# The end of an adaLN block: transposes of the last layernorm in another bank, the down product by four tiles, and a new order of the last block

## The chip, the cores and the metric

The kernel runs on one core of one Trainium2 chip. A core has five engines, each with its own queue of instructions: TensorE (PE; its weight loads are shown apart as PEld), VectorE (DVE), ScalarE (ACT), GpSimd (POOL) and SyncE (SP, which here only issues transfers). Engines wait for each other through semaphores. The metric is the device time of one execution in microseconds (us); of several runs the median is given. Three runs of the kernel before took 1085.74, 1085.96 and 1087.61 us, so its median is 1085.96 us.

## The reference

One transformer block in fp32 with adaptive layernorm, on x of shape (2, 1024, 256). From a small vector c come six rows per batch: shifts and scales for two layernorms, and two gates.

```python
h = _layernorm(x, axis=-1) * (1 + ca) + sa
x = x + ga * attention(h)          # 16 heads of 128, rotary positions, causal softmax, biases
h = _layernorm(x, axis=-1) * (1 + cb) + sb
x = x + gb * ffn(h)
```

The feed-forward part is `down(silu(gate(h)) * up(h))` with a hidden width of 704; its three weights are integers with a zero point and a scale per row. 704 is five chunks of 128 and one of 64.

## The kernel before, in words

**The main loop.** A unit is one head of one batch; there are 32. For each unit the loop projects q, k and v, forms the causal scores of eight query tiles of 128 rows in two-bank tiles of PSUM (pool `ps_sc`, two buffers), takes the softmax on VectorE and ScalarE, transposes the probabilities, multiplies by v and adds the output projection to x, which stays in SBUF. Nothing of this loop is touched by the change. The order of all work is written out by hand (`tc.manual_schedule`, L646): each engine executes its instructions in the order in which the Python code emits them, and the framework adds the waits.

**The end.** After the last unit (from L737) the two batches go through the feed-forward part in four blocks of 512 rows, named (batch, block): (0,0), (0,1), (1,0), (1,1). What a block needs:

- Layernorm: `ln_stats`, `ln_sqrt`, `ln_scale` give normalised tiles `xn_b` (128 rows by 256). `ln_turn` (L206) turns four of them: for each half f of the 256 columns four transposes on TensorE (L210) into one bank of `ps_a`, then one VectorE instruction (L217) that scales and shifts into h. It is called for the blocks (1,0) and (1,1) at the end, and twice, with ScalarE for the second half, at the kernel's start.
- `hidden(b, blk, c)` (L525) computes chunk c of the hidden layer: gate and up products (L538) into one two-bank tile `pgu` of `ps_sc`, a SiLU on ScalarE (L557), a product on VectorE (L558) into `gT`. The sixth chunk (c = 5) holds gate in 64 rows and up in the other 64 of one product, and its VectorE work (L553) writes even row tiles to partitions 0 to 63 of `gT` and odd ones to 64 to 127.
- `down(b, blk, *js)` (L560) forms the output of row tiles js: for each tile five products over 128 rows (L566), then for all js one product over the remaining 64 rows (L575, on the lower or the upper 64 rows of the array by the tile's parity), then an addition of x on VectorE (L588) into a tile `yo` and a store issued by SP (L589). The `yo` tiles of block (0,0) come from a pool of two buffers, all others from the pool of `xn`, with four.

**Banks.** `bank` (L496) hands out single banks in turn: `ps_y`, `ps_o`, `ps_a`, `ps_a`. The late output projections (`project_out(..., late=True)`, whose reader on VectorE is L512) and all `pd` tiles of `down` use it. `ps_a` has two buffers, which `ln_turn` uses as well.

**The order at the end.** `hidden(0,1,5)`; `ln_turn` for (1,0); statistics of the last four tiles; `down(0,0)` of tiles 0 and 1; `ln_scale`; `down(0,0)` of tiles 2 and 3; `ln_turn` for (1,1); then the six chunks of (1,0) with `down(0,1)` of all four tiles behind chunk 3; the six chunks of (1,1) with `down(1,0)` behind chunk 3; `down(1,1)` in two pairs of tiles.

Of the kernel before, what the change touches and what calls it, by code (L numbers as in the profile page):

```python
# [11 lines left out]
F32 = mybir.dt.float32  # L12
I32 = mybir.dt.int32
AF = mybir.ActivationFunctionType
ALU = mybir.AluOpType
PSUM = bass.MemoryType.PSUM

P = 128
B, S, D = 2, 1024, 256
H, DH = 16, 128  # L20
HID = 704
NT = S // P
KC = D // P
HG = 2
NG = H // HG
NF = (HID + P - 1) // P
FULL = (HID // P) * P
QB = 512
# [9 lines left out]
def adaln_block(ctx: ExitStack, tc: tile.TileContext, a, cos_d, sin_d, out):  # L38
    nc = tc.nc
# [4 lines left out]
    xnp = pool("xn", 4)  # L44
    fpool = pool("f", 2)
    rot = pool("rot", 2)
    ps_a = pool("ps_a", 2, space=PSUM)
    ps_o = pool("ps_o", 1, space=PSUM)
    ps_y = pool("ps_y", 1, space=PSUM)
    ps_sc = pool("ps_sc", 2, space=PSUM)  # L50
# [3 lines left out]
    x = [const.tile([P, NT, D], F32, name=f"x{b}") for b in range(B)]  # L54
    x_d = a["L0_attn_x"]
    R_BQ, R_BK, R_BV = 0, H, 2 * H
    cols = const.tile([P, 3 * H], F32, name="cols")
    sc = const.tile([P, B, KC], F32, name="sc")
# [8 lines left out]
    for n in range(KC):  # L67
        load_x(0, 2 * n, 2, nc.sync)
        half = slice(n * D, (n + 1) * D)
# [3 lines left out]
    ident = const.tile([P, P], F32, name="ident")  # L73
# [10 lines left out]
    for n in range(3):  # L84
# [10 lines left out]
        out=mask[:, NT - 1, :],  # L95
# [92 lines left out]
    def ln_sqrt(b, name, t0, t1):  # L188
        mv, rstd = stats[b, name]
        nc.scalar.activation(rstd[:, t0:t1], mv[:, t0:t1, 1], AF.Sqrt, bias=eps_t)  # L190

    xns = {}

    def ln_scale(b, name, blk, part=range(4)):
        mv, rstd = stats[b, name]
        part = [4 * blk + j for j in part]
        some = slice(part[0], part[-1] + 1)
        nc.vector.reciprocal(rstd[:, some], rstd[:, some])
        for t in part:
            xn = xnp.tile([P, D], F32, tag="xn", name=f"xn_{name}{b}_{t}")  # L200
            nc.vector.tensor_scalar(
                xn, x[b][:, t, :], mv[:, t, 0:1], rstd[:, t : t + 1], ALU.subtract, ALU.mult
            )
            xns[b, name, t] = xn

    def ln_turn(b, name, blk, which, dest, split=False):  # L206
        for f in range(KC):
            pt = ps_a.tile([P, 512], F32, tag="a", name=f"ptx_{name}{b}_{blk}_{f}")
            for j in range(4):
                nc.tensor.transpose(  # L210
                    pt[:, ts(j, P)], xns[b, name, 4 * blk + j][:, ts(f, P)], ident
                )
            shift, scale = (modT[:, which + n, f, b : b + 1] for n in range(2))
            if split and f:
                nc.scalar.activation(dest[:, f, :], pt, AF.Identity, bias=shift, scale=scale)
            else:
                nc.vector.tensor_scalar(dest[:, f, :], pt, scale, shift, ALU.mult, ALU.add)  # L217

    moved = {}

# [34 lines left out]
    wdT = [const.tile([P, NF, D], F32, name=f"wdT{b}") for b in range(B)]  # L255
# [240 lines left out]
    def bank(name):  # L496

        pool, tag = banks[turn[0] % 4]
        turn[0] += 1
        return pool.tile([P, 512], F32, tag=tag, name=name)  # L500
# [16 lines left out]
    h2s, gTs = {}, {}  # L517

    def new_h2(b, blk):

        tag = (f"hT{blk}", f"cs{blk}")[b]
        h2s[b, blk] = hpool.tile([P, KC, QB], F32, tag=tag, name=f"h2_{b}{blk}")
        return h2s[b, blk]

    def hidden(b, blk, c, late=True):  # L525
        if c == 0:
            gTs[b, blk] = fpool.tile([P, NF, QB], F32, tag="f", name=f"gT_{b}{blk}")
        last = c == NF - 1
        if late:
            pg = ps_sc.tile([P, S], F32, tag="sc", name=f"pgu_{b}{blk}{c}")  # L530
            pgs = [pg[:, ts(j, QB)] for j in range(2)]
        else:
            pgs = [
                ps_a.tile([P, 512], F32, tag="a", name=f"pgu_{b}{blk}{c}{j}") for j in range(2 - last)
            ]
        for pg, n in zip(pgs, ("gate",) if last else ("gate", "up")):
            for k in range(KC):
                nc.tensor.matmul(  # L538
                    pg,
                    wT["last"][:, k, :] if last else wT[n][:, k, ts(c, P)],  # L540
                    h2s[b, blk][:, k, :],
                    start=(k == 0),
                    stop=(k == KC - 1),
                )
        sg = ppool.tile([P, QB], F32, tag="p", name=f"sg_{b}{blk}{c}")
        if last:

            m = HID - FULL
            nc.scalar.activation(sg[m:], pgs[0][:m], AF.Silu)

            for j, rows_ in enumerate((slice(0, m), slice(m, P))):
                part = lambda t: t.rearrange("p (t j q) -> p t j q", j=2, q=P)[:, :, j, :]
                nc.vector.tensor_tensor(  # L553
                    part(gTs[b, blk][rows_, c, :]), part(sg[m:]), part(pgs[0][m:]), ALU.mult
                )
        else:
            nc.scalar.activation(sg, pgs[0], AF.Silu)  # L557
            nc.vector.tensor_tensor(gTs[b, blk][:, c, :], sg, pgs[1], ALU.mult)  # L558

    def down(b, blk, *js):  # L560

        pds = {}
        for j in js:
            pds[j] = bank(f"pd_{b}{blk}{j}")
            for c in range(NF - 1):
                nc.tensor.matmul(  # L566
                    pds[j][:, :D],
                    gTs[b, blk][:, c, ts(j, P)],
                    wdT[b][:, c, :],
                    start=(c == 0),  # L570
                    stop=False,
                )
        for j in js:
            half = ts(j % 2, HID - FULL)
            nc.tensor.matmul(  # L575
                pds[j][:, :D],
                gTs[b, blk][half, NF - 1, ts(j, P)],
                wdT[b][half, NF - 1, :],
                start=False,
                stop=True,  # L580
            )
        for j in js:
            t = blk * 4 + j
            if (b, blk) == (0, 0):
                yo = rot.tile([P, D], F32, tag="r1", name=f"yo_{b}{t}")
            else:
                yo = xnp.tile([P, D], F32, tag="xn", name=f"yo_{b}{t}")
            nc.vector.tensor_tensor(yo, pds[j][:, :D], x[b][:, t, :], ALU.add)  # L588
            nc.sync.dma_start(out[b, ts(t, P), :], yo)  # L589


    units = [(b, g, h) for b in range(B) for g in range(NG) for h in range(HG)]
# [53 lines left out]
    with tc.manual_schedule():  # L646
# [30 lines left out]
        ln_scale(0, "a", 0, (2, 3))  # L677
        shift_scale(0)
        ln_turn(0, "a", 0, 0, new_hT(0, 0), split=True)
        for t in range(4, NT):  # L680
            ln_stats(0, "a", t)
# [5 lines left out]
        ln_scale(0, "a", 1)  # L687
        release()
        ln_turn(0, "a", 1, 0, new_hT(0, 1), split=True)
        gates()  # L690
        for s in ("q", "k"):
# [3 lines left out]
        for n, u in enumerate(units):  # L695
            b, g, h = u
# [4 lines left out]
            for i in range(NT):  # L701
# [26 lines left out]
                if not nxt and i < NF:  # L728
                    hidden(0, 0, i, late=False)
# [9 lines left out]
        for c in range(4):  # L739
            hidden(0, 1, c)  # L740
            project_out(prev, 4 + c, late=True)
            project_out(u, c, late=True)
# [4 lines left out]
        values(u, 1, 0, 8)  # L747
        ln_scale(1, "b", 0)
        hidden(0, 1, 4)
        for t in range(4, NT):  # L750
            project_out(u, t, late=True)
        hidden(0, 1, 5)
        ln_turn(1, "b", 0, 2, new_h2(1, 0))
        for t in range(4, NT):
            ln_stats(1, "b", t)
        ln_sqrt(1, "b", 4, NT)
        down(0, 0, 0, 1)
        ln_scale(1, "b", 1)
        down(0, 0, 2, 3)
        ln_turn(1, "b", 1, 2, new_h2(1, 1))  # L760
        for c in range(NF):
            hidden(1, 0, c)
            if c == 3:
                down(0, 1, 0, 1, 2, 3)
        for c in range(NF):
            hidden(1, 1, c)
            if c == 3:
                down(1, 0, 0, 1, 2, 3)
        down(1, 1, 0, 1)
        down(1, 1, 2, 3)  # L770


def _rotary_tables():
# [65 lines left out]
```

## Time and profile before

| what | value |
|---|---|
| median of three runs | 1085.96 us (1085.74 to 1087.61) |
| the profiled execution's own time | 1085.72 us |
| its span in the profile | 1083.9 us |
| TensorE busy | 1072.0 us, 99% of the span |
| VectorE, ScalarE, GpSimd busy | 60%, 47%, 37% |
| granted TensorE clock | 1.00 |
| the four blocks' end, from `ln_turn` for (1,0) on | 999.73 to 1083.9 us |

The profile is of one execution. A row of a timeline gives its start and its length in us, the engine, the line of the kernel, the operation with what it writes and reads, how many instructions are merged in it, and in brackets how long the engine stood idle before and for whom. [...] the pace of TensorE is the distance from one start to the next. An fp32 product is two records in the trace, each with a weight load of its own.

### The profile page before, as it was taken

What the parts mean: (1) busy time and instruction counts of PE and PEld (TensorE: products, weight loads), DVE (VectorE), ACT (ScalarE), POOL (GpSimd) and SP (SyncE); (2) the same over time, 40 slices, a digit from 0 to 9 for tenths busy, and PEclk for the clock granted to TensorE, in tenths of its full rate; (3) what the DMA queues carried; (4) which work ended last, traced back from release to release, by engine and by line L of the source; (5) the groups of instructions that cost most, each with busy time, mean ns of one, the idle gap of its engine ahead of it and who ended that gap; (6) DMA issues with size and microseconds to landing.
All of it is one profiled execution on the core that took longest, in us unless ns stands there. A gap on an engine that the chain in (4) does not pass through costs nothing.

```text
span 1083.9 us, 12352 instructions
## 1 busy us (share of the span) xinstructions
PE 1072.0 (99%) x3524; PEld 638.7 (59%) x3524; DVE 655.5 (60%) x1422; ACT 507.6 (47%) x956; POOL 397.2 (37%) x364
## 2 busy tenths in 40 slices
PE   8999999999999999999999999999999999999998
PEld 5556555566666556556566666665655566555656
DVE  5566566767677856556656665666677766454321
ACT  4645445455445444445455444454445445652110
POOL 4635353535343343664343433333333334100000
PEclk9999999999999999999999999999999999999999
DMA  6355656657564556555564645454556556422001
GB/s 211 81 140 132 159 141 137 168 116 182 127 150 96 131 120 151 126 128 143 111 148 106 151 109 141 101 138 101 142 117 153 117 123 143 97 66 51 20 20 39
DMA packets 67191, 130.97 MB, mean 121 GB/s; under 512 B 18962, under 2 KB 23314, under 8 KB 67124
## 3 DMA queue, kind: packets, MB, share of 16 engines
q1 hardware_dynamic: 64772, 125.91, 49.1%
q10 hardware_dynamic: 2304, 4.16, 1.2%
q8 instruction: 28, 0.46, 0.2%
q14 instruction: 39, 0.32, 0.1%
q0 software_dynamic: 48, 0.13, 0.1%
HBM read 25.26 MB, written 2.10 MB: 25 GB/s over the span
## 4 chain that ended last, share of the span: by engine, by line
PE 95%; DVE 2%; SPq 1%; DMA 1%; ACT 1%; issue 0%; DVEq 0%; ACTq 0%
PE po L483 23%; PE ps L422 22%; PE pk L379 10%; PE pq L379 10%; PE py L509 10%; PE pv L361 10%; PE pgu L538 6%; PE pd L566 3%; SPq L468 1%; DMA pT<-t 1%; DMA wmod<-in_wmod 0%; PE pd L575 0%; ACT L557 0%; DVE ps L425 0%; DVE t L456 0%
## 5 line engine op out<-in xcount | busy, mean ns | idle before, releaser
L442 ACT ACTIVATE p<-ps,nmax 128x128 f32<-128x128 f32 (+7 forms) x256 | 189.8, 741 | 421.6 <-DVE nmax L425 421.5
L422 PE MATMUL ps<-kT,qT 128*128 128x512 f32 (+3 forms) x768 | 289.5, 486 | 0.7 <-ACT p L442 0.7
L425 DVE CUSTOM_DVE_ANT_0 ps<-ps,mask 128x128 f32<-128x128 f32 (+7 forms) x256 | 195.6, 764 | 132.9 <-PE ps L422 132.6
L483 PE MATMUL po<-pT,v 128*128 128x512 f32 (+3 forms) x768 | 264.0, 487 | 1.7 <-DMA pT<-t 1.6
L512 DVE SCALAR_TENSOR_TENSOR x<-py,rden,x 128x256 f32<-128x256 f32 x256 | 123.0, 482 | 182.9 <-PE py L509 176.2
L483 PEld LDWEIGHTS po<-pT,v 128*128 128x128 f32 x768 | 145.2, 190 | 133.0 <-issue 107.5
L456 DVE STREAM_TRANSPOSE t<-p 128x128 f32<-128x128 f32 (+7 forms) x256 | 198.1, 774 | 0.4 <-ACT p L442 0.4
L422 PEld LDWEIGHTS ps<-kT,qT 128*128 128x128 f32 x768 | 145.7, 190 | 77.5 <-issue 62.9
L392 POOL TENSOR_TENSOR r_k<-r_k,sin_t 128x512 f32<-128x512 f32 x64 | 81.4, 1272 | 223.0 <-ACT r_k L391 222.9
L509 PE MATMUL py<-wo,o 128*128 128x256 f32 x512 | 151.5, 380 | 1.4 <-DVE x L512 1.4
L392 POOL TENSOR_TENSOR r_q<-r_q,sin_t 128x512 f32<-128x512 f32 x64 | 81.7, 1276 | 140.3 <-ACT r_q L391 137.3
L398 POOL TENSOR_TENSOR kT<-kT,r_k 128x512 f32<-128x512 f32 x64 | 81.3, 1270 | 140.9 <-DVE rden L506 101.5
L509 PEld LDWEIGHTS py<-wo,o 128*128 128x128 f32 x512 | 92.3, 190 | 67.3 <-issue 51.2
L361 PE MATMUL pv<-wv,hT 128*128 128x256 f32 x512 | 121.0, 379 | 1.1 <-DVE qT L395 1.1
L379 PE MATMUL pq<-hT,wq 128*128 128x512 f32 x256 | 120.6, 593 | 0.5 <-DVE hT L217 0.5
L379 PE MATMUL pk<-hT,wk 128*128 128x512 f32 x256 | 120.3, 592 | 0.0
L361 PEld LDWEIGHTS pv<-wv,hT 128*128 128x128 f32 x512 | 94.9, 190 | 19.9 <-DVE qT L395 1.2
L391 ACT ACTIVATE r_q<-pq,cols 64x512 f32<-64x512 f32 x128 | 87.4, 683 | 20.9 <-PE pq L379 19.2
L398 POOL TENSOR_TENSOR qT<-qT,r_q 128x512 f32<-128x512 f32 x64 | 83.6, 1306 | 31.1 <-DVE qT L395 28.6
L391 ACT ACTIVATE r_k<-pk,cols 64x512 f32<-64x512 f32 x128 | 87.4, 683 | 6.2 <-PE pk L379 0.4
L379 PEld LDWEIGHTS pk<-hT,wk 128*128 128x128 f32 x256 | 48.6, 190 | 54.6 <-issue 44.0
L379 PEld LDWEIGHTS pq<-hT,wq 128*128 128x128 f32 x256 | 46.1, 190 | 33.8 <-issue 31.2
(89 smaller groups left out, 688.8 us busy)
## 6 DMA issues: line engine op xcount, KB each, us to landing
pT<-t SPq DMA_DIRECT2D x512, 128.0 KB, 2.4
pT<-t SPq DMA_DIRECT2D x512, 64.0 KB, 2.0
wq<-in_Wq SPq DMA_DIRECT2D x16, 256.0 KB, 3.1
wk<-in_Wk SPq DMA_DIRECT2D x16, 256.0 KB, 4.0
wv<-in_Wv SPq DMA_DIRECT2D x16, 256.0 KB, 4.2
wo<-in_Wo SPq DMA_DIRECT2D x16, 256.0 KB, 2.9
out<-yo SPq DMA_DIRECT2D x16, 128.0 KB, 1.8
x<-in_x SPq DMA_DIRECT2D x4, 256.0 KB, 5.4
```

The source lines that it names most:

```text
L361: nc.tensor.matmul(pv[:, ts(j, HG * DH)], hT[b, n][:, k, ts(r, P)], weights[b, g]["v"][:, k, :], start=(k == 0), stop=(k == KC - 1),)
L379: nc.tensor.matmul(pq, weights[b, g][s][:, k, ts(h, DH)], hT[b, n][:, k, :], start=(k == 0), stop=(k == KC - 1),)
L391: nc.scalar.activation(r1[to], pq[of], AF.Identity, bias=cols[of, c : c + 1])
L392: nc.gpsimd.tensor_tensor(r1, r1, sin_t[:, sl], ALU.mult)
L398: nc.gpsimd.tensor_tensor(dst[:, sl], dst[:, sl], r1, ALU.add)
L422: nc.tensor.matmul(ps[:, c:e], qT[:, ts(i, P)], kT[:, c:e], start=True, stop=True)
L425: nc.vector.tensor_tensor_reduce(ps[:, :L], ps[:, :L], mask[:, NT - 1 - i :, :].rearrange("p t k -> p (t k)"), -SCALE, FLT_MAX, ALU.add, A ...
L442: nc.scalar.activation(p[:, :L], ps[:, :L], AF.Exp, bias=nmax, scale=-1.0, accum_out=dens[u][:, i : i + 1])
L456: nc.vector.transpose(t32[blk][:, :, j, : i + 1, :].rearrange("p c k b -> p k c b"), p[:, : (i + 1) * P].rearrange("p (k c a) -> p k c a", ...
L483: nc.tensor.matmul(po[:, off * P :], vs[b, g][:, k, ts(h, DH)], pT[:, off:, :, k, :], start=(k == 0), stop=(k == last),)
L509: nc.tensor.matmul(py[:, :D], outs[u][:, ts(t, P)], weights[b, g]["o"][:, h, :], start=True, stop=True)
L512: nc.vector.scalar_tensor_tensor(x[b][:, t, :], py[:, :D], rdens[u][:, t : t + 1], x[b][:, t, :], ALU.mult, ALU.add)
```

## The change

It has four parts.

1. `ln_turn` can take one two-bank tile of the scores' pool (`wide`) in place of two banks of `ps_a`; the call for (1,0) does. In all calls both halves' tiles are now taken first, and the readers are emitted behind all eight transposes.
2. `down` treats all four row tiles in one call, for every block. Block (0,0) was done in two pairs before; `ln_scale` of the last four tiles now stands ahead of it.
3. `ln_turn` for (1,1) is called behind chunk 0 of (1,0) and not ahead of it.
4. In block (1,1) chunk 5 of the hidden layer is computed first, `down(1,0)` follows the third further chunk in that order, and `down(1,1)` starts with the 64-row products of all tiles. Each tile then gets its five 128-row products, its addition and its store before the next tile is begun. The fourth tile is split into two parts of 128 columns, the second in a bank of the scores' pool; each part has its own addition and store.

```diff
-    def ln_turn(b, name, blk, which, dest, split=False):
+    def ln_turn(b, name, blk, which, dest, split=False, wide=False):
+        tag = f"ptx_{name}{b}_{blk}"
+        if wide:
+            both = ps_sc.tile([P, S], F32, tag="sc", name=tag)
+            pts = [both[:, ts(f, QB)] for f in range(KC)]
+        else:
+            pts = [ps_a.tile([P, 512], F32, tag="a", name=f"{tag}_{f}") for f in range(KC)]
         for f in range(KC):
-            pt = ps_a.tile([P, 512], F32, tag="a", name=f"ptx_{name}{b}_{blk}_{f}")
             for j in range(4):
                 nc.tensor.transpose(
-                    pt[:, ts(j, P)], xns[b, name, 4 * blk + j][:, ts(f, P)], ident
+                    pts[f][:, ts(j, P)], xns[b, name, 4 * blk + j][:, ts(f, P)], ident
                 )
+        for f in range(KC):
...
-    def hidden(b, blk, c, late=True):
-        if c == 0:
+    def hidden(b, blk, c, late=True, first=None):
+        if c == 0 if first is None else first:
...
-    def down(b, blk, *js):
+    def down(b, blk):
+
+        end = (b, blk) == (1, 1)
+        pds = [bank(f"pd_{b}{blk}{j}") for j in range(4)]
+
+        parts = [(j, pds[j], slice(0, D)) for j in range(4)]
+        if end:
+            rest = ps_sc.tile([P, S], F32, tag="sc", name=f"pd_{b}{blk}r")
+            parts[3:] = [(3, pds[3], slice(0, P)), (3, rest, slice(P, D))]
+
+        def halves():
+            for j, pd, cols in parts:
+                half = ts(j % 2, HID - FULL)
+                nc.tensor.matmul(
+                    pd[:, cols],
+                    gTs[b, blk][half, NF - 1, ts(j, P)],
+                    wdT[b][half, NF - 1, cols],
+                    start=end,
+                    stop=not end,
+                )
+
+        def chunks(j, pd, cols):
             for c in range(NF - 1):
                 nc.tensor.matmul(
-                    pds[j][:, :D],
+                    pd[:, cols],
                     gTs[b, blk][:, c, ts(j, P)],
-                    wdT[b][:, c, :],
-                    start=(c == 0),
-                    stop=False,
+                    wdT[b][:, c, cols],
+                    start=(c == 0 and not end),
+                    stop=(c == NF - 2 and end),
                 )
...
+        def store(j, pd, cols):
             t = blk * 4 + j
...
+            nc.vector.tensor_tensor(yo[:, cols], pd[:, cols], x[b][:, t, cols], ALU.add)
+            nc.sync.dma_start(out[b, ts(t, P), cols], yo[:, cols])
+
+        yos = {}
+        if end:
+
+            halves()
+            for part in parts:
+                chunks(*part)
+                store(*part)
+            return
+        for part in parts:
+            chunks(*part)
+        halves()
+        for part in parts:
+            store(*part)
...
-        ln_turn(1, "b", 0, 2, new_h2(1, 0))
+        ln_turn(1, "b", 0, 2, new_h2(1, 0), wide=True)
         for t in range(4, NT):
             ln_stats(1, "b", t)
         ln_sqrt(1, "b", 4, NT)
-        down(0, 0, 0, 1)
         ln_scale(1, "b", 1)
-        down(0, 0, 2, 3)
-        ln_turn(1, "b", 1, 2, new_h2(1, 1))
+        down(0, 0)
         for c in range(NF):
             hidden(1, 0, c)
+            if c == 0:
+                ln_turn(1, "b", 1, 2, new_h2(1, 1))
             if c == 3:
-                down(0, 1, 0, 1, 2, 3)
-        for c in range(NF):
-            hidden(1, 1, c)
-            if c == 3:
-                down(1, 0, 0, 1, 2, 3)
-        down(1, 1, 0, 1)
-        down(1, 1, 2, 3)
+                down(0, 1)
+        order = (NF - 1, *range(NF - 1))
+        for c in order:
+            hidden(1, 1, c, first=(c == order[0]))
+            if c == order[3]:
+                down(1, 0)
+        down(1, 1)
```

More of the change, by code (lines that the diff above doesn't have):

```diff
@@ L204, in ln_scale @@
             xns[b, name, t] = xn
-    def ln_turn(b, name, blk, which, dest, split=False):
+    def ln_turn(b, name, blk, which, dest, split=False, wide=False):
[5 more added lines that the diff above has]
+            pts = [ps_a.tile([P, 512], F32, tag="a", name=f"{tag}_{f}") for f in range(KC)]
         for f in range(KC):
-            pt = ps_a.tile([P, 512], F32, tag="a", name=f"ptx_{name}{b}_{blk}_{f}")
             for j in range(4):
                 nc.tensor.transpose(
-                    pt[:, ts(j, P)], xns[b, name, 4 * blk + j][:, ts(f, P)], ident
+                    pts[f][:, ts(j, P)], xns[b, name, 4 * blk + j][:, ts(f, P)], ident
                 )
+        for f in range(KC):
             shift, scale = (modT[:, which + n, f, b : b + 1] for n in range(2))
             if split and f:
-                nc.scalar.activation(dest[:, f, :], pt, AF.Identity, bias=shift, scale=scale)
+                nc.scalar.activation(dest[:, f, :], pts[f], AF.Identity, bias=shift, scale=scale)
             else:
-                nc.vector.tensor_scalar(dest[:, f, :], pt, scale, shift, ALU.mult, ALU.add)
+                nc.vector.tensor_scalar(dest[:, f, :], pts[f], scale, shift, ALU.mult, ALU.add)
     moved = {}
@@ L558, in hidden @@
             nc.vector.tensor_tensor(gTs[b, blk][:, c, :], sg, pgs[1], ALU.mult)
-    def down(b, blk, *js):
-        pds = {}
-        for j in js:
-            pds[j] = bank(f"pd_{b}{blk}{j}")
+    def down(b, blk):
[16 more added lines that the diff above has]
+        def chunks(j, pd, cols):
@@ L565, in down @@
             for c in range(NF - 1):
                 nc.tensor.matmul(
-                    pds[j][:, :D],
+                    pd[:, cols],
                     gTs[b, blk][:, c, ts(j, P)],
-                    wdT[b][:, c, :],
-                    start=(c == 0),
-                    stop=False,
-                )
[L573 to L581, printed above, removed]
@@ L582, in down @@
-        for j in js:
-            t = blk * 4 + j
[L584 to L589, printed above, removed]
+                    wdT[b][:, c, cols],
+                    start=(c == 0 and not end),
+                    stop=(c == NF - 2 and end),
+                )
@@ new lines, in store @@
+        def store(j, pd, cols):
+            t = blk * 4 + j
+            if cols.start == 0:
+                if (b, blk) == (0, 0):
+                    yos[t] = rot.tile([P, D], F32, tag="r1", name=f"yo_{b}{t}")
+                else:
+                    yos[t] = xnp.tile([P, D], F32, tag="xn", name=f"yo_{b}{t}")
+            yo = yos[t]
+            nc.vector.tensor_tensor(yo[:, cols], pd[:, cols], x[b][:, t, cols], ALU.add)
+            nc.sync.dma_start(out[b, ts(t, P), cols], yo[:, cols])
```

## The prediction

> **What bounds the kernel now.** I read the page first: which engine is full, and on which engine the chain that ended last lies.
>
> ```profile
> span 1083.9 us, 12352 instructions
> PE 1072.0 (99%) x3524; PEld 638.7 (59%) x3524; DVE 655.5 (60%) x1422; ACT 507.6 (47%) x956; POOL 397.2 (37%) x364
> ...
> PE 95%; DVE 2%; SPq 1%; DMA 1%; ACT 1%; issue 0%; DVEq 0%; ACTq 0%
> ```
>
> TensorE is busy 99% and carries 95% of the chain, so time can only be won where TensorE waits, where its own work shrinks, or after its last product. The change touches only the last 90 us, so next I read the timeline of TensorE there (start, length, what; [...] the pace is read from start to start).
>
> ```profile
> 997.09 1.88 PE L538 MATMUL pgu<-h,wlastT 128*128 128x512 f32 x4
> 999.73 1.09 PE L210 MATMUL ptx_b<-ident,xn_b 128*128 128x128 f32 x8 [0.76 <-DVE x L512]
> 1000.66 4.48 PE L566 MATMUL pd<-wdT,gT 128*128 128x256 f32 x20
> 1005.07 0.70 PE L575 MATMUL pd<-wdT,gT 64*128 64x256 f32 x4
> 1005.71 4.58 PE L566 MATMUL pd<-wdT,gT 128*128 128x256 f32 x20
> 1010.22 0.70 PE L575 MATMUL pd<-wdT,gT 64*128 64x256 f32 x4
> 1011.43 1.09 PE L210 MATMUL ptx_b<-ident,xn_b 128*128 128x128 f32 x8 [0.51 <-DVE yo L588]
> 1012.36 1.88 PE L538 MATMUL pgu<-h,wgateT 128*128 128x512 f32 x4
> ...
> 1026.10 8.80 PE L566 MATMUL pd<-wdT,gT 128*128 128x256 f32 x40
> 1034.83 1.13 PE L575 MATMUL pd<-wdT,gT 64*128 64x256 f32 x8
> 1035.89 1.98 PE L538 MATMUL pgu<-h,wgateT 128*128 128x512 f32 x4
> 1037.71 1.88 PE L538 MATMUL pgu<-h,wupT 128*128 128x512 f32 x4
> ```
>
> The two bracketed waits are the only idle of TensorE in this stretch; both stand before the transposes `ptx_b`, whose banks of `ps_a` still hold tiles that VectorE has to read. Each fp32 product is two records: four records of 512 columns take 1.72 (0.43 each), records of 256 take 0.215. The two ways of writing `down` are side by side: in pairs (1000.66 to 1010.86, if the last four 64-row records take 0.64 like the first four) and four at once (1026.10 to 1035.89).
>
> Third, the end: the timeline of all engines after the last products, then the landing times of the stores in the answer on the tile `yo`.
>
> ```profile
> 1079.48 0.70 PE L575 MATMUL pd<-wdT,gT 64*128 64x256 f32 x4
> 1080.21 0.76 DVE L588 TENSOR_TENSOR yo<-pd,x 128x256 f32<-128x256 f32 x2 [4.39 <-PE pd L575]
> ...
> 1080.66 0.81 SPq L589 DMA_DIRECT2D out<-yo  x2
> ...
> DMA to landing us min/median/max: 1.7/1.8/2.0
> ```
>
> TensorE ends at 1080.18; two additions, two issues, a landing and the closing make 3.72 us to 1083.9.
>
> [...] here loads of neighbouring records start 0.11 apart. [...] two records of 128 columns of `po` start at 991.71 and the next group at 991.93, 0.11 each; eight transposes take 0.93, 0.117 each. [...] eight 64-row records fill 1.06, half of 8 x 0.215 plus 0.2. [...]
>
> **The change, part by part**, on the clock of the profile before.
>
> *First transposes to a bank of the scores.* They now wait for `pgu` of chunk 4 of block (0,1), read by the DVE product that ran 997.53 to 998.22. TensorE comes free at 997.09 + 1.72 = 998.81, 0.6 later. So they start at 998.81 instead of 999.73: **-0.92**. The first `down` tile then starts at 999.74; its banks were freed by the four L512 additions, which end about 998.8, 999.2, 999.7 and 1000.1, in the order in which the tiles want them, so no wait comes in its place. `xn_b` is long done (last about 991.9).
>
> *down(0,0) by four tiles.* 8.73 + 1.06 = 9.79 (as at 1026.10) instead of 1011.43 - 1000.66 = 10.77: **-0.98**, of which 0.57 is the idle before the second transposes and 0.41 one change to 64 rows and back less. Added: the first products behind the 64-row group take 1.82 instead of 1.72 (1035.89 to 1037.71): **+0.10**.
>
> *Second transposes one chunk on.* Same 0.93. What they wait for moves: `yo` of tiles 2 and 3 must free `ps_a`. The `yo` tiles of this block have two buffers, so the third addition waits for the first store. Group at 1008.47; first `yo` 0.73 later (as 1034.83 to 1035.56), 1009.20; store issued 0.45 later, 1009.65; landed by 1011.65 at the slowest; third `yo` done 1012.1, fourth 1012.5. TensorE reaches the transposes at 1009.53 + 1.82 + 1.72 = 1013.07, and their second half 0.47 later: about 1 us to spare. Behind the waiting addition on VectorE stand the fourth, then gT of chunk 0, whose sigmoid comes only after 1013.07 + 1.28 (table load) + 0.60; nothing is held. ln_scale ahead of `down` on VectorE ends by about 1006.6 (its root is there at 1005.0, then 0.17 + 1.38), before any `yo`. The h rows (1.53 us) land behind gT of chunk 0, near 1017.3; their readers come 20 us later. Up to here -1.80: chunk 1 starts at 1014.00 instead of 1015.80.
>
> *Chunk 5 of block (1,1) first.* Two half chunks (1.72 each) are now neighbours, so chunk 0 of (1,1) needs the bank of chunk 5 of (1,0). From the rows of before: its two L553 products end at 1042.82, its turn comes at 1041.14 + 1.72 = 1042.86, and a weight load takes 0.05 after the release to start and 0.11 to be ready: **+0.12** (bounds 0 and 0.35). Before, a full chunk of 3.44 lay between.
>
> *down(1,1).* Before: 1069.92 to 1080.18, 10.26. After: entering 64 rows 0.1; the group 1.06 to 1.28 (one more product, on the same half as its neighbour; I take 1.15); 30 records of 256: 6.45 + 0.10; 20 records of 128: at 0.11 to 0.117 each, the last 0.27 long, 2.36 to 2.5. Sum 10.07 to 10.4: **-0.1** (bounds -0.2 and +0.15). The gT wait of chunk 4 (ready 1.5 after its products) is covered: TensorE reads it 1.1 + 8 x 0.215 = 2.8 after. The extra bank, of the scores, was freed by gT of chunk 3, some 2 us before. In the two calls of `ln_turn` at the kernel's start the reads move behind all eight transposes in the text only; the order on each engine stays, so 0.
>
> *The tail.* One addition of 128 columns: 416 ns at 256 and 688 at 512 give 0.28. It ends 0.31 after TensorE instead of 0.79, and its issue need not stand behind another: 0.45 less. From issue to the end 2.80 (1081.10 to 1083.9), by estimate 0.1 to 0.2 less for half the bytes. **-0.6** (bounds -0.4 and -0.7). One more issue on SP (0.37) lies a microsecond before the last.
>
> Sum: -0.92 - 0.98 + 0.10 + 0.12 - 0.10 - 0.60 = **-2.38**. Span 1081.5; the profiled execution's 1085.72 becomes 1083.3. It stands 0.24 under the median 1085.96 of the runs, so I forecast 1083.6.
>
> **The rivals.**
> 1. *Only the idle goes.* The merge of groups and the narrow last part give nothing (a change of rows costs elsewhere, the last landing is as long), or the second transposes find `ps_a` taken: -1.49 + 0.22 and perhaps -0.2: about 1084.6. For it: these are small sums of modelled ends. Against: both forms of `down` stand in the trace.
> 2. *Slower: the narrow products.* Twenty records of 128 columns in a row, each with its own load. If load and stream do not overlap in a long run (0.19 + 0.11 = 0.30 each), down(1,1) is 3.7 longer: 1087.3. It decides from 0.237 each (2.4 / 20 above 0.117). Against: transposes run eight in a row at 0.117.
> 3. *The change doesn't act*, because the wait for the score bank ends as late as that for `ps_a`: then 0.92 is missing, 1084.5. Against: that bank's reader ended at 998.22.
>
> **How the numbers follow.** Forecast as summed 0.80; rivals 1 and 3 together 0.14; rival 2 and unseen mishaps 0.06. Bounds of the unknown terms, with the scatter of the medians (before: 1085.74 to 1087.61), make the main case 1083.0 to 1084.3; the range, 1082.8 to 1085.0, takes in rivals 1 and 3. A measurement of this kernel tells about 0.2%, 2.2 us, from no change; the sum lies just above it. Of the 0.80 about 0.53 is beyond 2.2; so faster 0.54, within 0.2% 0.40, slower 0.06.
>
> **What would show it.** No bracket before either `ptx_b`; down(0,0) as one row of 40 and one of 8; chunk 1 of (1,0) 1.8 earlier; at chunk 0 of (1,1) a DVE wait of TensorE of about 0.1; the narrow records 0.11 apart; 3.1 us from the last product to the end. A `ptx_b` wait on `yo` or a pace of 0.2 for the narrow records would make me wrong.

## The result, and the profile after

The changed kernel takes 1083.66 us (median of 14 runs, 1081.58 to 1087.26), the kernel before 1085.87 us (14 runs, 1084.2 to 1087.61): ratio 0.9978, 95% interval 0.9969 to 0.9987. So it is faster by 0.22%, or 2.2 us, and the interval reaches from 0.13% to 0.31%. The profiled execution took 1082.3 us with a span of 1080.5 us.

The page of the changed kernel, its span and engines:

```profile
span 1080.5 us, 12377 instructions
PE 1071.1 (99%) x3536; PEld 639.6 (59%) x3536; DVE 656.3 (61%) x1423; ACT 507.6 (47%) x956; POOL 397.1 (37%) x364
```

The timeline of TensorE in the part that was changed (start, length, engine, line, operation, instructions merged):

```profile
996.26 1.88 PE L544 MATMUL pgu<-h,wlastT 128*128 128x512 f32 x4
997.98 1.04 PE L215 MATMUL ptx_b<-ident,xn_b 128*128 128x128 f32 x8
998.85 8.80 PE L589 MATMUL pd<-wdT,gT 128*128 128x256 f32 x40
1007.58 1.13 PE L579 MATMUL pd<-wdT,gT 64*128 64x256 f32 x8
1008.64 1.98 PE L544 MATMUL pgu<-h,wgateT 128*128 128x512 f32 x4
1010.46 1.88 PE L544 MATMUL pgu<-h,wupT 128*128 128x512 f32 x4
1012.18 1.04 PE L215 MATMUL ptx_b<-ident,xn_b 128*128 128x128 f32 x8
1013.05 1.88 PE L544 MATMUL pgu<-h,wgateT 128*128 128x512 f32 x4
...
1036.68 3.60 PE L544 MATMUL pgu<-h,wlastT 128*128 128x512 f32 x8
1040.23 1.96 PE L544 MATMUL pgu<-h,wgateT 128*128 128x512 f32 x4
1042.02 1.88 PE L544 MATMUL pgu<-h,wupT 128*128 128x512 f32 x4
...
1065.65 1.88 PE L544 MATMUL pgu<-h,wupT 128*128 128x512 f32 x4
1067.46 1.13 PE L579 MATMUL pd<-wdT,gT 64*128 64x256 f32 x8
1068.22 0.38 PE L579 MATMUL pd_11r<-wdT,gT 64*128 64x128 f32 x2
1068.53 7.86 PE L589 MATMUL pd<-wdT,gT 128*128 128x256 f32 x40
1076.23 1.28 PE L589 MATMUL pd_11r<-wdT,gT 128*128 128x128 f32 x10
```

Neither `ptx_b` row has a bracket any more: TensorE does not wait before them. `down(0,0)` is one row of 40 records and one of 8. The two half chunks (`wlastT`) stand together as one row of 8, and the next row starts 3.55 later, not 3.44. The row of the ten narrow records of `pd_11r` is 1.28 long. A row can be longer than the way to the next start: the four records of 512 columns at 1010.46 are 1.88 long, and the next row starts 1.72 after them began.

The spans differ by 3.4 us, but not all of that belongs to the change. The products of chunk 5 of block (0,1), the last work that both kernels do in the same way, start at 997.09 before and at 996.26 after: 0.83 was won in the main loop, whose instructions are the same. What the change is worth is read from that point to the end of the span, and I call this **the stretch**: 1083.9 - 997.09 = 86.81 before, 1080.5 - 996.26 = 84.24 after, 2.57 less. The span is printed to a tenth, so a stretch is good to about 0.05 and a difference of two to about 0.1. The traces keep the spans to the nanosecond (1083.915 and 1080.527 us, which make the gain 2.56); where a tenth decides, I give what they say.

### The profile page after: what moved, and what is told of

Same layout as the page of the kernel before. It is cut to its first block, busy times and chain, and to the rows that moved or that the text cites. A ratio compares the mean times of both kernels' runs of the same rounds, so it can differ in the third digit from the quotient of the medians.

```text
span 1080.5 us, 12377 instructions
## 1 busy us (share of the span) xinstructions
PE 1071.1 (99%) x3536; PEld 639.6 (59%) x3536; DVE 656.3 (61%) x1423; ACT 507.6 (47%) x956; POOL 397.1 (37%) x364
## 4 chain that ended last, share of the span: by engine, by line
PE 95%; DVE 1%; DMA 1%; SPq 1%; ACT 1%; issue 0%; DVEq 0%; ACTq 0%
PE po L489 23%; PE ps L428 22%; PE pk L385 10%; PE py L515 10%; PE pq L385 10%; PE pv L367 10%; PE pgu L544 7%; PE pd L589 3%; SPq L474 1%; DMA pT<-t 1%; DMA x<-in_x 0%; PE pd L579 0%; DVE ps L431 0%; ACT L563 0%; DVE xn_a L201 0%
```

## The experiments

Unless it says otherwise, each kernel is the changed one with one edit, and its verdict is read from the stretch of its own profile; where no time is given, it was executed once, under the profiler. None leaves any work out.

### The first transposes back in `ps_a`

```diff
-        ln_turn(1, "b", 0, 2, new_h2(1, 0), wide=True)
+        ln_turn(1, "b", 0, 2, new_h2(1, 0))
```

> The changed kernel with its first part undone: the transposes for (1,0) go to two banks of ps_a again. Read from the start of the chunk-5 products of block (0,1) to the end of the span: 86.81 us before, 84.24 us changed. Theory (the bank is what TensorE waited for): the wait of about 0.8 for L518 is back, the transposes start 2.64 behind those products and not 1.72, the stretch is 85.2. Rival (the score bank is no freer): 84.2.

Stretch 1082.6 - 997.32 = 85.28. The timeline of TensorE shows where the 1.04 more lie (0.98 with the spans to the nanosecond):

```profile
997.32 1.88 PE L544 MATMUL pgu<-h,wlastT 128*128 128x512 f32 x4
999.96 1.09 PE L215 MATMUL ptx_b<-ident,xn_b 128*128 128x128 f32 x8 [0.77 <-DVE x L518]
1000.89 8.80 PE L589 MATMUL pd<-wdT,gT 128*128 128x256 f32 x40
```

The transposes start 2.64 behind the chunk-5 products, as in the kernel before, and wait for the same addition. The bank was the cause of 0.92; 0.06 more comes from the transposes themselves: behind a wait they take 0.93 to the next start, without one 0.87. In the profile of the changed kernel their first weight load starts at 997.55, 0.43 before they do; in that of the kernel before, behind the wait, it starts with them, at 999.73.

### `down(0,0)` in pairs again

```diff
-        def halves():
-            for j, pd, cols in parts:
+        def halves(some):
+            for j, pd, cols in some:
...
-            halves()
+            halves(parts)
...
-        for part in parts:
-            chunks(*part)
-        halves()
-        for part in parts:
-            store(*part)
+        groups = [parts[:2], parts[2:]] if (b, blk) == (0, 0) else [parts]
+        for group in groups:
+            for part in group:
+                chunks(*part)
+            halves(group)
+            for part in group:
+                store(*part)
```

> The changed kernel with block (0,0) of down in two pairs of tiles again, all else as changed. Theory (each change to 64 rows and back costs TensorE about 0.3 to 0.4 even without any wait): down(0,0) takes 10.2 instead of 9.79, the stretch 84.65. Rival (only the idle before the second transposes was won): 9.8 and 84.25.

Stretch 1082.4 - 997.71 = 84.69. On the timeline of TensorE:

```profile
1000.30 4.48 PE L589 MATMUL pd<-wdT,gT 128*128 128x256 f32 x20
1004.71 0.70 PE L579 MATMUL pd<-wdT,gT 64*128 64x256 f32 x4
1005.34 4.58 PE L589 MATMUL pd<-wdT,gT 128*128 128x256 f32 x20
1009.86 0.70 PE L579 MATMUL pd<-wdT,gT 64*128 64x256 f32 x4
1010.49 1.98 PE L544 MATMUL pgu<-h,wgateT 128*128 128x512 f32 x4
```

The same 48 records take 10.19 and not 9.79, with no bracket anywhere. So one more change to 64 rows and back cost 0.40 of pure TensorE time here. What rival 1 of the prediction said of the merge, that it brings nothing, is out.

### The second transposes back ahead of chunk 0

```diff
         down(0, 0)
+        ln_turn(1, "b", 1, 2, new_h2(1, 1))
         for c in range(NF):
             hidden(1, 0, c)
-            if c == 0:
-                ln_turn(1, "b", 1, 2, new_h2(1, 1))
```

> The changed kernel with its third part undone: the transposes for (1,1) stand ahead of chunk 0 of (1,0) again, behind down by four tiles. Theory (they wait for the third and fourth yo, and these for the first stores of a pool of two buffers): a wait of about 2.4 for yo before ptx_b, stretch 86.7, ratio to before about 1.000. Rival (the wait is the one of before, for the additions alone): 0.6 to 0.8, stretch 85.0, ratio 0.998.

The wait is as expected, and the stretch is not: 1083.7 - 995.50 = 88.20. The ratio to the kernel before is 1.001 (1.000 to 1.002): without its third part the change does not gain. The timeline of TensorE:

```profile
1006.82 1.14 PE L579 MATMUL pd<-wdT,gT 64*128 64x256 f32 x8
1010.34 1.97 PE L215 MATMUL ptx_b<-ident,xn_b 128*128 128x128 f32 x8 [2.38 <-DVE yo L605]
1012.10 2.56 PE L544 MATMUL pgu<-h,wgateT 128*128 128x512 f32 x4
1014.50 1.88 PE L544 MATMUL pgu<-h,wupT 128*128 128x512 f32 x4
```

The wait of 2.38 is there. But the transposes behind it take 1.76 to the next start and not 0.93, and the gate products 2.40 and not 1.72: 1.5 more that no wait explains. Busy times by window of the same profile say why (start and end, length in us, then busy time and instructions of TensorE, its weight loads, VectorE, ScalarE and GpSimd, then the granted TensorE clock, the busy share of the DMA engines and their GB/s):

```profile
1008.00:1010.00 2.00, 0.00 (x0) 0.00 (x0) 0.45 (x2) 0.00 (x0) 0.00 (x0) 1.00 0.40 131
1010.00:1013.00 3.00, 2.66 (x10) 2.15 (x11) 2.17 (x4) 0.00 (x0) 0.00 (x0) 0.51 0.27 87
1013.00:1014.00 1.00, 1.00 (x3) 0.48 (x2) 0.16 (x1) 0.00 (x0) 0.00 (x0) 0.77 0.00 0
1014.00:1016.00 2.00, 2.00 (x6) 0.95 (x5) 0.00 (x0) 0.00 (x0) 0.00 (x0) 1.00 0.00 0
```

Near the end of the idle the granted clock fell to 0.50 (1.00 from 1009.4 to 1009.8, 0.50 from 1010.1 to 1010.3), and it came back to 1.00 only after 1013.4 (0.50 from 1013.2 to 1013.4, 0.86 in the next 0.2, then 1.00). TensorE worked from 1010.34 to about 1013.4 at that clock, and half of these 3.1 is the other 1.5. Not every execution paid it: of the kernel's 12 runs three had a mean clock of 1.000 and took 1085.41, 1085.44 and 1085.63 us. The nine others, 1085.45 to 1090.21 us, had means of 0.997 or 0.998, and the profiled one, with its fall, is among them with 0.998; but 5 of the 14 runs of the changed kernel have such means too, so the runs do not say how many of the nine paid it here.

### The same, with buffers enough for `yo`

Here the third and fourth `yo` of block (0,0) are taken from two other buffers, so that all four additions can run without a store having landed.

```diff
-                if (b, blk) == (0, 0):
+                if (b, blk) == (0, 0) and j < 2:
                     yos[t] = rot.tile([P, D], F32, tag="r1", name=f"yo_{b}{t}")
+                elif (b, blk) == (0, 0):
+                    yos[t] = small.tile([P, D], F32, tag="bw", name=f"yo_{b}{t}", bufs=2)
...
         down(0, 0)
+        ln_turn(1, "b", 1, 2, new_h2(1, 1))
         for c in range(NF):
             hidden(1, 0, c)
-            if c == 0:
-                ln_turn(1, "b", 1, 2, new_h2(1, 1))
```

> As the run with the second transposes back ahead of chunk 0, but the third and fourth yo of block (0,0) have two buffers of their own, so that no addition waits for a store. Theory (the landing of the first stores makes 1.6 of the wait): the wait before ptx_b shrinks from 2.4 to about 0.8, stretch 85.05. Rival: the wait stays at 2.4.

Stretch 1082.9 - 997.90 = 85.0. TensorE's timeline:

```profile
1009.22 1.13 PE L579 MATMUL pd<-wdT,gT 64*128 64x256 f32 x8
1011.10 1.09 PE L215 MATMUL ptx_b<-ident,xn_b 128*128 128x128 f32 x8 [0.74 <-DVE yo L607]
1012.03 1.88 PE L544 MATMUL pgu<-h,wgateT 128*128 128x512 f32 x4
```

The wait shrank from 2.38 to 0.74, and the gate products take 1.72 again. So 1.64 of the 2.38 was the landing of the first stores, and 0.74 the additions alone. The merge into one group of four had made the two buffers of `yo` matter; chunk 0 in between covers both terms.

### The last tile whole

```diff
-        if end:
-            rest = ps_sc.tile([P, S], F32, tag="sc", name=f"pd_{b}{blk}r")
-            parts[3:] = [(3, pds[3], slice(0, P)), (3, rest, slice(P, D))]
```

> The changed kernel with the fourth tile of down(1,1) whole: one part of 256 columns, one addition, one store. From the start of the chunk-5 products of (0,1) to the end: 84.24 changed. Theory (the narrow last part pays behind the products: addition 0.29 instead of 0.42, landing 1.5 instead of 1.8, against 0.1 more on TensorE): 84.55. Rival (the narrow products cost what the tail saves): 84.2 or less.

Stretch 1082.3 - 997.87 = 84.43, 0.19 more than the changed kernel (0.15 with the spans to the nanosecond), about half of the 0.31 that was expected. The end in this kernel, TensorE's last row, then the last addition and store:

```profile
1070.13 8.90 PE L586 MATMUL pd<-wdT,gT 128*128 128x256 f32 x40
...
1079.07 0.42 DVE L602 TENSOR_TENSOR yo<-pd,x 128x256 f32<-128x256 f32 x1 [1.73 <-PE pd L586]
1079.53 0.33 SPq L603 DMA_DIRECT2D out<-yo  x1
```

and in the changed kernel, the last addition, with the landing time of its two narrow stores from the list of issues:

```profile
1077.55 0.29 DVE L605 TENSOR_TENSOR yo<-pd_11r,x 128x128 f32<-128x128 f32 x1 [0.82 <-PE pd_11r L589]
...
out<-yo SPq DMA_DIRECT2D x2, 64.0 KB, 1.5
```

Whole, the products end 8.90 after their start, split 8.98 (1068.53 to 1077.51): the narrow records cost 0.08. Behind the products, whole takes 1082.3 - 1079.03 = 3.27, split 1080.5 - 1077.51 = 2.99: 0.28 won (0.23 to the nanosecond: the last store is issued 0.13 earlier, and from there to the end it is 2.66 instead of 2.76, 0.10 less where 0.3 was expected of the landing). So the split is worth only 0.15 to 0.2 of the 2.57. The larger part of the shorter end, 3.72 to 3.27, is won here without the split: each tile has its own addition and store, and the last tile's addition and store have no other to wait behind. Rival 2 is out: the narrow records start 0.11 apart ((1.28 - 0.28) / 9 in the row of ten, a record of its own being 0.28 long).

### Chunk 5 last, its products in `down(1,1)` first

```diff
-        order = (NF - 1, *range(NF - 1))
+        order = tuple(range(NF))
```

> The changed kernel with the chunks of (1,1) in the order 0 to 5 and the 64-row products of down(1,1) first all the same. Theory (these products need chunk 5 of gT, 1.3 to 1.7 behind its products on TensorE): a wait of TensorE of 1.2 to 1.7 before L579, no wait at chunk 0 of (1,1) (0.18 less): stretch 85.3 to 85.8. Rival (ScalarE and VectorE keep up, the order of the chunks is free): 84.06.

Stretch 1083.4 - 997.67 = 85.73. TensorE's timeline:

```profile
1066.87 1.88 PE L544 MATMUL pgu<-h,wlastT 128*128 128x512 f32 x4
1069.88 1.37 PE L579 MATMUL pd<-wdT,gT 64*128 64x256 f32 x8 [1.14 <-DVE gT L559]
1071.10 0.38 PE L579 MATMUL pd_11r<-wdT,gT 64*128 64x128 f32 x2
1071.41 7.86 PE L589 MATMUL pd<-wdT,gT 128*128 128x256 f32 x40
```

TensorE waits for the even half of `gT`, and then, inside the group, for the odd half: 1.53 from 1069.88 to 1071.41 where the changed kernel takes 1.07. The order of the chunks is what lets the 64-row products go first; the rival falls. The two half chunks are no neighbours here, and their 0.18 is gone as well.

### Chunk 5 second

```diff
-        order = (NF - 1, *range(NF - 1))
+        order = (0, NF - 1, *range(1, NF - 1))
```

> The changed kernel with chunk 5 of (1,1) behind its chunk 0, so that the two half chunks are no neighbours. Theory (the two half chunks in a row cost 0.18, since the bank comes free 1.7 behind a half chunk and TensorE is there after 1.72): the wait at chunk 0 is gone, stretch 84.06. Rival (the cost sits elsewhere, or moves on to chunk 1): 84.24.

Stretch 1081.0 - 996.93 = 84.07. TensorE's timeline:

```profile
1037.36 1.88 PE L544 MATMUL pgu<-h,wlastT 128*128 128x512 f32 x4
1039.08 1.88 PE L544 MATMUL pgu<-h,wgateT 128*128 128x512 f32 x4
1040.79 1.88 PE L544 MATMUL pgu<-h,wupT 128*128 128x512 f32 x4
1042.51 1.88 PE L544 MATMUL pgu<-h,wlastT 128*128 128x512 f32 x4
1044.22 1.88 PE L544 MATMUL pgu<-h,wgateT 128*128 128x512 f32 x4
```

Every row starts 1.71 or 1.72 behind the one before. The 0.18 that the two neighbours cost is gone, and no wait took its place.

### The first three parts alone

The order of the chunks and `down(1,1)` in pairs are those of the kernel before.

```diff
-        end = (b, blk) == (1, 1)
+        end = False
...
-        order = (NF - 1, *range(NF - 1))
+        order = tuple(range(NF))
...
+        groups = [parts[:2], parts[2:]] if (b, blk) == (1, 1) else [parts]
...
```

> Only the first three parts of the change; order of the chunks and down(1,1) in two pairs as before. Theory (parts add): 1.92 of the 2.57 are won in front, stretch 84.9, ratio to before about 0.9982. Rival (the front gain is given back when the end keeps its old form): 86 or more.

```profile
span 1083.9 us, 12349 instructions
...
999.03 1.88 PE L544 MATMUL pgu<-h,wlastT 128*128 128x512 f32 x4
```

Stretch 1083.9 - 999.03 = 84.87; ratio to the kernel before 0.9987 (0.9978 to 0.9996). The stretch says that 1.94 of the 2.57 come from the first three parts, and 0.63 from the fourth (1.91 and 0.65 to the nanosecond). The times alone could not have said it: their interval holds 0.9982 and much else.

### Both side by side

The kernel with chunk 5 second, and the changed kernel unaltered, timed on one chip.

> The changed kernel with chunk 5 of (1,1) behind its chunk 0, timed beside the unaltered changed kernel. Theory: the stretch from the chunk-5 products of (0,1) to the end is 84.06 again, 2.75 less than before; ratio to before 0.9975; against the unaltered changed kernel 0.18 us less, which its scatter of some us from run to run will hide. Rival (the single look was luck): 84.24 or more.

> The changed kernel unaltered, as the measure for the run beside it. Theory (the scatter of the times comes from the main loop, where products of po wait for the transposed probabilities, and not from the end): the stretch is 84.24 within 0.05 whatever the run's own time; ratio to before 0.9978. Rival (the end itself scatters): the stretch differs by some tenths or more.

Chunk 5 second: stretch 1081.6 - 997.50 = 84.10, 1083.49 us (8 runs), ratio 0.9978 (0.9967 to 0.9988). Unaltered: stretch 1082.3 - 998.03 = 84.27, 1083.96 us (7 runs), ratio 0.9976 (0.9965 to 0.9986). The stretches repeat within 0.03 of the earlier ones (within 0.004 with the spans to the nanosecond) while the starts of the stretch differ by 1.8 (996.26 and 998.03 for one and the same kernel), so in these profiles the end itself does not scatter. Chunk 5 second is the better order by 0.17 in the trace (0.18 to the nanosecond, twice), and the times cannot tell the two apart.

## Why the prediction was right

It forecast 1083.6 us, and 1083.66 was measured. By its own steps, each as the prediction put it and as the trace has it, in us:

| step | forecast | measured | where |
|---|---|---|---|
| first transposes to a bank of the scores | -0.92 | -0.92 | 2.64 to 1.72 behind chunk 5; undone, 2.64 again |
| `down(0,0)` by four tiles | -0.98 | -0.98 | 10.77 to 9.79; the merge alone 0.40 |
| first products behind the 64-row group | +0.10 | +0.10 | 1.82 between starts |
| both transposes | 0 | -0.12 | 0.87 each instead of 0.93 |
| chunk 5 of (1,1) first | +0.12 | +0.18 | 1040.23 - 1036.68 and the next row, 5.34 instead of 5.16 |
| `down(1,1)` | -0.1 | -0.12 | 10.26 to 10.14, from 1067.37 (the last chunk's products over) to 1077.51 |
| the tail | -0.6 | -0.73 | 3.72 to 2.99 |
| sum | -2.38 | -2.57 | the stretch (the steps, rounded, give -2.59) |

Two rows belong beside the table: the start of `down(1,1)` in the profile before, and, from the profile after, the addition that could have held up the second transposes:

```profile
1069.92 4.48 PE L566 MATMUL pd<-wdT,gT 128*128 128x256 f32 x20
...
1010.62 0.91 DVE L605 TENSOR_TENSOR yo<-pd,x 128x256 f32<-128x256 f32 x2 [1.55 <-DMA out<-yo]
```

**Right in mechanism and size.** Both waits went as described, and no other of their size took their place. The two risks were costed rightly. The third `yo` waited for the first store and ended at 1010.62 + 0.42 = 1011.04, 1.1 before TensorE reached the second transposes (forecast 1012.1 and 1013.07, on a clock that runs 0.83 later); the narrow records run at the pace of the transposes, 0.11 against 0.117. One of the signs named beforehand did not show: no bracket for VectorE stands at chunk 0 of (1,1). That TensorE is held there is read from its starts, and from the two orders in which the 0.18 is gone.

**Sizes that were off.** The term "0" for the second transposes left out that transposes without a wait ahead take 0.87 and not 0.93: 0.06 each, twice. The first weight load starts 0.43 before both rows (997.55 and 997.98, 1011.75 and 1012.18). The term "+0.12" for the half chunks counted the delay of the first record behind them (0.11 measured), and not that the row which begins so late is itself longer: it takes 1.79 to the next start and not 1.72. The tail was taken too long: the last store is issued 0.36 behind the last product and not 0.91, which is 0.55 earlier where 0.45 was forecast, while from its issue to the end it is 2.66 instead of 2.83, inside the 0.1 to 0.2 less of the estimate. So -0.73 lies just past the bound of -0.7. All three are small; the first and the last made the forecast gain too small, the second too large.

**What was luck.** The median came within 0.06 us of the forecast, while the forecast summed 2.38 and the trace holds 2.57: the scatter of the two medians made up the difference. The measured interval, 0.13% to 0.31%, would have held a gain anywhere from 1.4 to 3.4 us. The forecast put 0.40 on less than 0.2%; that was a fair doubt, for the measured 0.22% is as close to the bound as the sum was, and the interval reaches to both sides of it.

**The rivals.** "Only the idle goes" falls with the pairs (0.40 without any wait) and the whole last tile (0.15 to 0.2). "The narrow products" falls with the pace of 0.11. "The change doesn't act" falls with the bank undone (the wait of 0.77 is back).

## What to carry to other kernels

When an edit is worth some us of a thousand, measure it in the trace from the last common instruction on: here the stretch repeats within 0.03 in the two kernels profiled twice, while the runs scatter over several us. Merging groups of work saved the changes between them (0.40 here) but makes all buffers come free at once; look for the pool that was large enough only because the work came in two halves (here the two `yo` buffers: 2.38 of wait without the third part of the change, 0.74 with two more buffers, nothing with a chunk of other work in between). Two short pieces of work should not be neighbours when they share a pool of two buffers: a buffer then comes free later than the next user wants it (here 0.18 for the two half chunks).

## What the runs showed of the hardware

**In one profile TensorE's granted clock fell to half in an idle of 2.38 us.** With the second transposes back, it read 1.00 up to 1009.8 and 0.50 from 1010.1 to 1013.4, while the idle lasted to 1010.34; that cost 1.5 us on top of the wait. In the windows around the waits of 0.77 and 1.14 in other kernels it read 1.00; behind the wait of 0.74 the gate products kept their 1.72 to the next start, and the mean clock of that execution is 1.000. A longer wait stands in the main loop of the kernel with the first three parts alone (us in total, times, the longest):

```profile
PE po L489 <- DMA pT<-t: 4.0, 4, 2.1
```

All windows of 60 us of that profile up to 1020 read 1.00; in the profile with the fall the one from 960 to 1020 reads 0.97. These are the two longest waits of TensorE in the twelve profiles, 2.38 with a fall and 2.1 without; what decides was not shown.

**One more change to 64 rows and back cost 0.40 us**, as the profiles with one and with two groups of 64-row products in `down(0,0)` show (9.79 and 10.19 for the same 48 records).

**The main loop scatters.** In the twelve profiles the chunk-5 products of block (0,1) start anywhere from 995.50 to 999.03, though the instructions up to there are the same. The start goes with the time that the products `po` wait in the main loop, for the transfer of the transposed probabilities or for nothing that the profile shows: 0.8 us in total at 995.50, 1.3 at 996.26, 1.6 at 997.09, 2.7 at 997.67, 3.0 at 997.90, 4.0 at 999.03. It is not exact (1.9 at 998.03), and no run here changed these transfers, so this is a likely cause and not a shown one. Runs without a profile may have a second one: in the 14 of the changed kernel, the five with a mean clock of 0.998 or less took 1083.89 to 1087.26 us, the nine others 1081.58 to 1084.30. No profile of the changed kernel caught such a run.
